# Gated cross-attention with a mixture of experts: seven half-size products for the experts' second layer, and two moves in the issue order

## The chip, the cores and the metric

The kernel runs on one core of a Trainium2 chip. The metric is device time in microseconds of one execution, given as the median of several runs. A core has five engines that each work through their own instructions in order and meet at semaphores: TensorE (PE in the profile, with its weight loads as PEld), VectorE (DVE), ScalarE (ACT), GpSimd (POOL) and SyncE (SP, which here only issues DMAs). All data is float32.

## The reference, cut to what matters

There are 4 x 1024 tokens of width 256, and a context of 64 rows for each of the 4 batches. The first half is a cross-attention with 16 heads of width 64, gated and added to x. The second half is a mixture of 8 experts with a hidden width of 1024: each token goes to its best two.

```python
# attention: per head, softmax(q k^T) v * q, then the projection
attn = softmax(einsum('hblk,hbmk->hblm', qh, kh))
out = einsum('hblm,hbmk->hblk', attn, vh) * qh
x = x + tanh(g_xattn) * (out.reshape(...) @ w_proj.T + b_proj)
# experts: top 2 of 8, weights from a softmax of the two logits
h = silu(einsum('td,edf->tef', xt, w1))      # 256 -> 1024
y = einsum('tef,efd->ted', h, w2)            # 1024 -> 256
x = x + tanh(g_ffn) * einsum('ted,te->td', y, combine)
```

The kernel computes only the two chosen experts of each token: tokens are sorted by expert into lists, and each run of list entries with one expert is a *slot*.

## The kernel before, in words

**Attention.** The tokens are cut into 8 groups (g = 0 to 7) of 512, a group into 4 tiles of 128. The main loop runs `for g in range(NG + 3): for t in range(T)`, and a pair (g, t) is called a step here. A step of the first eight groups issues the scores of its tile (`sc`, L385), the softmax (maximum L394, subtraction L396, exponential L399, sum L401, reciprocal L402, and the last multiplication `pr` on POOL, L404), and then the transposes of the *previous* step's probabilities (`pa`, L414). In step 1 of each group the attention product of the group before follows (`po`, L428, multiplied into `qT` on DVE at L437), in steps 2 and 3 its projection (`pp`, L445). Two groups later the second layer norm runs (`norm_again`), transposes `pt_b` (L281, copied by ACT at L286), the gate's logits `pl` (L467) and `pl_t` (L477).

**Routing.** After every second group, routing has found for each of 8 tiles of 128 tokens to which row of the lists its two entries go. `enter` writes them by indirect DMAs on POOL, two for a tile (L568). The function `entries(g, part)` issues 6 such writes at the last step of a group, 6 and 4 at the first two steps of the next. After the lists of groups 0 to 3 a table of *early* slots is made (slots 0 to 8), after those of groups 4 to 7 the table of *late* slots.

**Slots.** A generator, `run_slots`, issues the experts' work in small pieces; every `yield` ends one. For each slot s it gathers the tokens of slot s+3 (`gather_tokens`, POOL, L845), runs the hidden layer of slot s (`hidden`: `ph` on PE at L899, Silu on ACT at L907 into `hT`), transposes the tokens of slot s+1 (`transposed`: `pt` on PE, L867, copied by ACT to `xT`), and issues the second layer of slot s-1 (`combine`: products `py`, L978, with eviction and scaling on DVE, L966, an addition on POOL, L970, and a scatter to the output, L939; the output's old rows were gathered at L922). Loads of the next lists and weights are issued on SP between. Before the last slot's hidden layer, the second layer of the slot before it is issued. The table `pieces` says how many pieces go to which step of groups 6 to 10; what is left runs after the loop. `behind_softmax` puts a POOL instruction behind the newest multiplication `pr`.

Slots 0 to 8 hold 256 tokens. Of the late slots that run here, 9 to 15 hold 384 ("wide"), 16 to 20 hold 320 ("half": two tiles of 128 and one of 64) and 21 to 27 hold 256 ("plain"). A matmul call is for 128 columns of `hT` as weights and a row block of w2 (256 columns) as the moving operand; eight such calls, one for each 128 of the hidden width, make one tile of a slot's output. Each call leaves two records in the trace[...].

**Buffers.** PSUM has four single banks, handed out in turn by `bank(name)` (for `pt`, `pa`, `po`, `pp`, `pl`, `py` and others), and two double ones for scores and `ph`. The SBUF pool `soft`, tag "pr", has 2 buffers of 1024 float32 a partition; `npool`, tag "nT", has 4.

Of the kernel before, what the change touches and what calls it, by code (L numbers as in the profile page):

```python
# [8 lines left out]
F32 = mybir.dt.float32  # L9
I32 = mybir.dt.int32  # L10
AF = mybir.ActivationFunctionType
ALU = mybir.AluOpType
# [3 lines left out]
P = 128  # L16
# [5 lines left out]
def kernel(  # L22
# [13 lines left out]
    w2: bass.AP,  # L36
    out: bass.AP,
):

# [19 lines left out]
    nc = tc.nc  # L61
# [44 lines left out]
    def bank(name, spare=False):  # L106

        if spare:
            return ps2.tile([P, 2, 512], F32, tag="ps2", name=name)[:, 0]
        return ps1.tile([P, 512], F32, tag="ps1", name=name)  # L110
# [123 lines left out]
    def apart(tensor, dma, part=None, behind=()):  # L234

        writers = [writer for name in behind for writer in written[name]]
        tc.declare_no_dep(dma.ins, group=tensor, keep=writers, reason="different rows")
        tc.add_to_no_dep_group(tensor, dma.ins)
        for writer in writers:
            tc.add_manual_dep(  # L240
                dma.ins,
                writer.name,
                mybir.DependencyInfo(mybir.DependencyClass.Sync, mybir.DependencyReason.DATA),
                reason="rows of the part",
            )
        if part:
            written.setdefault(part, []).append(dma.ins)
# [589 lines left out]
    def behind_softmax():  # L837

        return tc.issue_after(newest[0]) if newest else nullcontext()
# [73 lines left out]
    def combine(s, ids, b, y, acc, hT):  # L913

        blocks = blocks_of(s)
        n = tokens_of(s)
        behind = [f"slot{s - 1}"] if s else ["out0"]
        if s == NA:
            behind.append("out1")
        for t, r in enumerate(blocks):  # L920
            with behind_softmax():
                gather = nc.gpsimd.indirect_dma_start(  # L922
                    out=acc[t][:r],
                    out_offset=None,
                    in_=outf[:n],
                    in_offset=bass.IndirectOffsetOnAxis(ap=ids[:r, t, 0:1], axis=0),
                    bounds_check=n - 1,
                    oob_is_err=False,
                )
            apart("out", gather, behind=behind)  # L930
        if attention_ends:
            py = [bank(f"py_{s}_{t}")[:, : D * r // P] for t, r in enumerate(blocks)]
        else:
            both = bank(f"py_{s}").rearrange("p (t d) -> p t d", d=D)
            py = [both[:, t, :] for t in range(blocks)]

        def scatter(t):
            r = blocks[t]
            put = nc.gpsimd.indirect_dma_start(  # L939
                out=outf[:n],  # L940
                out_offset=bass.IndirectOffsetOnAxis(ap=ids[:r, t, 0:1], axis=0),
                in_=acc[t][:r],
                in_offset=None,
                bounds_check=n - 1,
                oob_is_err=False,
            )
            apart("out", put, f"slot{s}")

        def parts_of(r):

            return [(slice(i * r, (i + 1) * r), slice(i * D * r // P, (i + 1) * D * r // P)) for i in range(P // r)]

        def add(t):
            r = blocks[t]
            last = s == NA + OFTEN - 1 and t == len(blocks) - 1
            if last:
                tc.keep_in_program_order(
                    nc.vector.scalar_tensor_tensor(
                        acc[t], py[t], ids.bitcast(F32)[:, t, 1:2], acc[t], ALU.mult, ALU.add
                    )  # L960
                )
                scatter(t)
                return

            for rows, columns in parts_of(r):
                evicted[s] = nc.vector.tensor_scalar(  # L966
                    y[t][:r, columns], py[t][rows], ids.bitcast(F32)[rows, t, 1:2], None, ALU.mult
                ).ins
            with behind_softmax():
                nc.gpsimd.tensor_tensor(acc[t][:r], acc[t][:r], y[t][:r], ALU.add)  # L970
                scatter(t)

        each = attention_ends
        per_tile = NF // len(hT)
        for t, r in enumerate(blocks):
            for f in range(NF):
                for rows, columns in parts_of(r):
                    nc.tensor.matmul(  # L978
                        py[t][rows],
                        hT[f // per_tile][:, f % per_tile, t * P : t * P + r],  # L980
                        b[:, f, columns],
                        start=(f == 0),
                        stop=(f == NF - 1),
                    )
            if each:
                add(t)
            yield
        if not each:
            for t in range(len(blocks)):
                add(t)  # L990
# [82 lines left out]
    def tabling(g):  # L1073

        nonlocal done, in_use
        if g == HG - 1:
            table, done = early_table()
            tables.append(table)
        elif g == NG - 1:
            table, in_use = late_table(done)  # L1080
            tables.append(table)

    def entries(g, part):
        nonlocal entered
        tiles = range(R)[3 * part : 3 * (part + 1)]
        with behind_softmax():
            enter(list(range(g - GB + 1, g + 1)), second["places"], tiles)
        entered += len(tiles)


    slots = run_slots(range(NA + OFTEN))
    pieces = {
        HG + 2: (0, 1, 1, 0), HG + 3: (3, 3, 2, 2), HG + 4: (3, 3, 3, 3), HG + 5: (1, 1, 2, 1), HG + 6: (1, 1),
    }
    last = None
    assert B * (H // 8) == 2 * T
# [12 lines left out]
    for g in range(NG + 3):  # L1109
        attention_ends = g >= NG  # L1110
        if g < NG:
            qT, aT = qTs[g], halves(f"aT_{g}", "hidden" if g % 2 and g + 1 < NG else "group")
            held[g] = (qT, aT)
        for h in parts[g]:
            if h == len(qTs):
                qTs.append(halves(f"qT_{h}"))
        before_last = g - 2
        ends = before_last % GB == GB - 1 and before_last >= 0
        for t in range(T):
            if g < NG:  # L1120
                pr = probabilities(g, t, qT)
            if last:
                transpose_probabilities(*last)
            if ends and t == 3:
                placing(before_last)
            products = [(h, p) for h, pairs in parts[g].items() for p in pairs[t]]
            if 0 < g <= NG and t == 1:
                for q in range(NP // 2):
                    attend(g - 1, q, *held[g - 1])
                    for h, p in products[q : q + 1]:  # L1130
                        queries(h, qTs[h], [p])
                products = products[NP // 2 :]
            for h, p in products:
                queries(h, qTs[h], [p])
            if 0 < g <= NG and t >= 2:
                project(g - 1, held[g - 1][0], (t - 2) * 2)
            last = (g, t, pr, aT) if g < NG else None
            if g == 0:
                for _ in range(value_parts[t]):
                    next(pending_values)  # L1140
            if 0 <= before_last < NG and t < 2:
                norm_again(before_last, t)
            if g + 2 < NG and t == 2:
                ln_norm(g + 2, stats, "a")
                add_bias(g + 2)
            if ends and t == 2:
                second["routing"] = route(second["logits"], f"{before_last}")
            if ends and t == 3:
                entries(before_last, 0)
            elif g >= GB + 2 and before_last % GB == 0 and t < 2:  # L1150
                entries(before_last - 1, t + 1)
                if t == 0:
                    tabling(before_last - 1)
            if g == 0 and t == 1:
                tc.keep_in_program_order(nc.scalar.activation(tg, tg, AF.Tanh))
                tc.keep_in_program_order(
                    nc.gpsimd.tensor_scalar(bias, bias, tg[:, 0:1], None, ALU.mult)
                )
                for h in range(2):
                    add_bias(h)  # L1160
            if g + 2 < NG and t == 0 and g % GB == 0:
                stats = ln_stats(list(range(g + 2, g + 2 + GB)), f"a{g + 2}")
            for _ in range(pieces[g][t] if g in pieces and t < len(pieces[g]) else 0):
                next(slots)
# [50 lines left out]
```

## Time and profile before

| what | value |
|---|---|
| time, median of 3 runs | 889.73 us (889.43 to 890.48) |
| the profiled execution's own time | 918.12 us |
| its span, from the first to the last instruction | 916.3 us |
| PE busy | 871.4 us (95%) |
| DVE, ACT, POOL busy | 327.8, 263.9, 403.0 us |
| second layer `py`, L978 | 1168 records, 238.3 us busy |
| hidden layer `ph`, L899 | 896 records, 233.8 us busy |
| list writes, L568 | 64, mean 971 ns |

The profiled execution took 28 us longer than the median of the timed runs, so a sum over its rows is a difference to itself, and how it carries over to the median has to be argued. PE is pipelined, so its busy time says that it had work, not that it ran at its peak. "Idle before" counts the time that an engine stood still just ahead of a group, with what released it. On the page, row 2 cuts the span into 40 slices of 22.9 us, and a digit is the busy share in tenths.

### The profile page before, as it was taken

How to read it: one execution, taken by the hardware profiler on the slowest of the kernel's cores; microseconds unless marked ns; L12 is line 12 of the kernel's file. 1: busy time of each engine (PE TensorE's matmuls, PEld its weight loads, DVE VectorE, ACT ScalarE, POOL GpSimd, SP SyncE). 2: the span in 40 equal slices, each digit the busy share in tenths (PEclk: the TensorE clock that was granted, in tenths of full speed). 3: DMA queues.
4: the chain of work that ended last, by engine and by line, in shares of the span. 5: the costliest groups of instructions: out<-in, count | busy, mean ns of one | idle time of the engine just before them, and what ended most of it. 6: DMA issues, size and time to landing. Idle time of an engine off the chain costs nothing.

```text
span 916.3 us, 11723 instructions
## 1 busy us (share of the span) xinstructions
PE 871.4 (95%) x4328; PEld 657.5 (72%) x4328; DVE 327.8 (36%) x729; ACT 263.9 (29%) x414; POOL 403.0 (44%) x392
## 2 busy tenths in 40 slices
PE   8999999999999998997997899999999999999995
PEld 5556858574857576865885787777777777888884
DVE  3467585777468748631155300000000001100010
ACT  4653353425242425432140121211211211121110
POOL 2051212146213553065447565555455555564443
PEclk9999999999999999998998899999999999999998
DMA  9600000001010225276372575744444564457111
GB/s 203 195 1 1 24 24 24 24 19 30 1 46 1 47 90 188 72 141 143 115 262 63 143 248 166 237 149 140 148 140 142 176 198 148 135 188 267 51 36 42
DMA packets 85279, 102.33 MB, mean 112 GB/s; under 512 B 29366, under 2 KB 71740, under 8 KB 85216
## 3 DMA queue, kind: packets, MB, share of 16 engines
q1 hardware_dynamic: 62656, 66.96, 24.4%
q0 software_dynamic: 11600, 25.25, 8.8%
q10 hardware_dynamic: 10960, 9.31, 3.7%
q8 instruction: 36, 0.59, 0.3%
q14 instruction: 27, 0.22, 0.1%
HBM read 84.75 MB, written 17.33 MB: 111 GB/s over the span
## 4 chain that ended last, share of the span: by engine, by line
PE 80%; DVE 10%; another core or an unknown queue 3%; issue 3%; DMA 1%; POOL 1%; ACT 1%; POOLq 0%; ACTq 0%; DVEq 0%
PE py L978 23%; PE ph L899 22%; PE pp L445 11%; PE pq L370 10%; PE sc L385 5%; PE pa L414 2%; PE pt L867 2%; PE po L428 2%; DVE qT L437 1%; PE pk L317 1%; DVE sm L401 1%; DVE pr L396 1%; DVE mx L394 1%; PE pt_b L281 1%
## 5 line engine op out<-in xcount | busy, mean ns | idle before, releaser
L978 PE MATMUL py<-w,hT 128*128 128x256 f32 (+1 forms) x1168 | 238.3, 369 | 9.2 <-issue 8.7
L899 PE MATMUL ph<-xT,w 128*128 128x256 f32 (+2 forms) x896 | 233.8, 418 | 2.1 <-ACT xT L872 1.2
L978 PEld LDWEIGHTS py<-w,hT 128*128 128x128 f32 (+1 forms) x1168 | 199.8, 184 | 40.2 <-issue 14.0
L899 PEld LDWEIGHTS ph<-xT,w 128*128 128x128 f32 x896 | 170.0, 191 | 57.5 <-issue 1.6
L907 ACT ACTIVATE hT<-ph 128x1024 f32<-128x1024 f32 (+3 forms) x84 | 69.9, 835 | 370.6 <-PE ph L899 319.5
L966 DVE TENSOR_SCALAR x<-py,ids 128x256 f32<-128x256 f32 (+1 forms) x72 | 33.5, 465 | 381.9 <-PE py L978 348.3
L404 POOL TENSOR_TENSOR pr<-pr,sm 128x1024 f32<-128x1024 f32 x32 | 60.9, 1902 | 218.1 <-DVE sm L402 202.1
L370 PE MATMUL pq<-nT_a,wq 128*128 128x512 f32 x256 | 117.0, 597 | 0.4 <-issue 0.2
L445 PE MATMUL pp<-wp,qT 128*128 128x256 f32 x512 | 113.2, 379 | 0.0
L445 PEld LDWEIGHTS pp<-wp,qT 128*128 128x128 f32 x512 | 97.0, 190 | 18.2 <-issue 5.3
L922 POOL DMA_INDIRECT x<-out_dram,ids x68 | 69.3, 1018 | 81.7 <-DMA out_dram<-x,ids 61.9
L845 POOL DMA_INDIRECT x<-normed,ids x68 | 67.9, 999 | 53.4 <-DMA ids<-lists 34.3
L970 POOL TENSOR_TENSOR x<-x,x 128x256 f32<-128x256 f32 (+1 forms) x67 | 48.3, 721 | 90.5 <-DVE x L966 77.8
L370 PEld LDWEIGHTS pq<-nT_a,wq 128*128 128x128 f32 x256 | 45.9, 190 | 53.5 <-issue 47.6
L939 POOL DMA_INDIRECT out_dram<-x,ids x68 | 69.0, 1015 | 23.2 <-POOL x L970 18.0
L568 POOL DMA_INDIRECT lists<-entry,to_row x64 | 62.1, 971 | 20.5 <-issue 17.9
L385 PEld LDWEIGHTS sc<-keys,qT 128*128 128x128 f32 x512 | 62.9, 192 | 7.9 <-issue 7.5
L385 PE MATMUL sc<-keys,qT 128*128 128x128 f32 x512 | 67.4, 278 | 0.0
L415 ACT COPY aT<-pa 128x512 f32<-128x512 f32 x64 | 34.6, 590 | 91.2 <-PE pa L414 71.1
L394 DVE TENSOR_REDUCE mx<-sc 128x16 f32<-128x1024 f32 x32 | 39.0, 1220 | 29.5 <-PE sc L385 28.3
L401 DVE TENSOR_REDUCE sm<-pr 128x16 f32<-128x1024 f32 x32 | 38.9, 1215 | 20.9 <-ACT pr L399 20.9
L377 ACT COPY qT<-pq 128x512 f32<-128x512 f32 x64 | 35.7, 582 | 28.4 <-PE pq L370 28.4
(209 smaller groups left out, 624.8 us busy)
## 6 DMA issues: line engine op xcount, KB each, us to landing
w<-in_L_ffn_w_dram SPq DMA_DIRECT2D x56, 1024.0 KB
out_dram<-x ACTq DMA_DIRECT2D x8, 512.0 KB
normed<-keep_b ACTq DMA_DIRECT2D x8, 512.0 KB
x<-in_x_dram SPq DMA_DIRECT2D x7, 512.0 KB
x<-normed,ids POOLq DMA_INDIRECT x68
x<-out_dram,ids POOLq DMA_INDIRECT x68
out_dram<-x,ids POOLq DMA_INDIRECT x68
wq<-in_L_xattn_w_qs_dram SPq DMA_DIRECT2D x4, 256.0 KB
```

The costliest lines, as they stand in the source:

```text
L370: nc.tensor.matmul(pq, wq[:, c, p * P : (p + 1) * P], nT[g][:, c, :], start=(c == 0), stop=(c == NC - 1),)
L385: nc.tensor.matmul(sc[:, p // 2, :, p % 2, :], of_pair(qT, p)[:, t * P : (t + 1) * P], kT[g // GB][:, p, :], start=True, stop=True,)
L404: nc.gpsimd.tensor_tensor(pr, pr, sm.unsqueeze(2).to_broadcast([P, H, M]), ALU.mult).ins
L445: nc.tensor.matmul(pp[:, i, :], of_pair(qT, p)[:, t * P : (t + 1) * P], wp[:, p, :], start=(p == 0), stop=(p == NP - 1),)
L568: nc.gpsimd.indirect_dma_start(out=lists, out_offset=bass.IndirectOffsetOnAxis(ap=to_row[:, k, i : i + 1], axis=0), in_=entry[:, k, i, :], ...
L845: gather = nc.gpsimd.indirect_dma_start(out=xin[t][:n], out_offset=None, in_=normed[: tokens_of(s)], in_offset=bass.IndirectOffsetOnAxis(a ...
L899: nc.tensor.matmul(ph[:, i, :], a[:, c, f * P : (f + 1) * P], xT[:, c, :], start=(c == 0), stop=(c == NC - 1),)
L907: nc.scalar.activation(hT[f0 // per_tile][:, f1 : f1 + step, :], ph, AF.Silu)
L922: gather = nc.gpsimd.indirect_dma_start(out=acc[t][:r], out_offset=None, in_=outf[:n], in_offset=bass.IndirectOffsetOnAxis(ap=ids[:r, t, 0 ...
L939: put = nc.gpsimd.indirect_dma_start(out=outf[:n], out_offset=bass.IndirectOffsetOnAxis(ap=ids[:r, t, 0:1], axis=0), in_=acc[t][:r], in_of ...
L970: nc.gpsimd.tensor_tensor(acc[t][:r], acc[t][:r], y[t][:r], ALU.add)
L978: nc.tensor.matmul(py[t][rows], hT[f // per_tile][:, f % per_tile, t * P : t * P + r], b[:, f, columns], start=(f == 0), stop=(f == NF - 1),)
```

## The change: what it does, and the diff

First, in slots 9 to 26 the two first tiles of the second layer (256 tokens x 1024 hidden by 1024 x 256) are cut into halves three ways: token tiles, the two halves of the hidden width, and the two halves of the output's columns. Eight products of quarter blocks become seven, by Winograd's form of Strassen's scheme: four sums of `hT` blocks (s1 to s4) and four of w2 blocks (t1 to t4) are made on DVE, seven products of four calls each at 128 columns go to one bank each, and the output's four blocks are put together from them on DVE by eight scaled additions, with two scaled copies on ACT. A third tile, where there is one, is done as before, and now ahead of the first two. Slot 27 is as before. The sums take buffers of the pools "pr" and "nT". The two POOL additions and scatters of the first two tiles come after product 3 and after product 4, the last.

Second, list writes: the tiles of a pair of groups go to a queue, `to_enter`, when their places are known, and each step takes one tile from it (two writes), or two tiles while the queue's first entry is of an odd-numbered pair of groups.

Third, `pieces`: the first pieces of the slots move one step on. In group 6 the generator's first two pieces go to steps 2 and 3 instead of 1 and 2; in group 7 the counts are (0, 4, 3, 3) instead of (3, 3, 2, 2). The totals are the same from the end of group 7 on.

```diff
+        whole = 2 if NA <= s < NA + OFTEN - 1 else 0
         if attention_ends:
-            py = [bank(f"py_{s}_{t}")[:, : D * r // P] for t, r in enumerate(blocks)]
+            py = [bank(f"py_{s}_{t}")[:, : D * r // P] if t >= whole else None for t, r in enumerate(blocks)]
...
+        def quarters():
+            half = NF // 2
+            if len(hT) == 2:
+                h = [[hT[k][:, :, i * P : (i + 1) * P] for k in range(2)] for i in range(2)]
...
+            w = [[b[:, k * half : (k + 1) * half, j * P : (j + 1) * P] for j in range(2)] for k in range(2)]
+            sums, more = (
+                soft.tile([P, 2, half, P], F32, tag="pr", name=f"{kind}_{s}") for kind in ("hsum", "wsum")
+            )
+            rest = npool.tile([P, 2, half, P], F32, tag="nT", name=f"rest_{s}")
+            s1, s2, s3, s4 = sums[:, 0], sums[:, 1], h[1][0], rest[:, 0]
+            t1, t2, t3, t4 = w[0][1], more[:, 0], rest[:, 1], more[:, 1]
+            for to, one, sign, other in (
+                (s1, h[1][0], ALU.add, h[1][1]),
+                (s3, h[0][0], ALU.subtract, h[1][0]),
+                (s2, s1, ALU.subtract, h[0][0]),
+                (s4, h[0][1], ALU.subtract, s2),
+                (t3, w[1][1], ALU.subtract, w[0][1]),
+                (t1, w[0][1], ALU.subtract, w[0][0]),
+                (t2, w[1][1], ALU.subtract, t1),
+                (t4, w[1][0], ALU.subtract, t2),
+            ):
+                nc.vector.tensor_tensor(to, one, other, sign)
...
+            def product(name, left, right):
+                to = bank(f"py_{s}_{name}")[:, :P]
+                n = NF // 2
+                for f in range(n):
+                    nc.tensor.matmul(to, left[:, f, :], right[:, f, :], start=(f == 0), stop=(f == n - 1))
+                return to
+
+            partial = work.tile([P, 2, P], F32, tag="xn", name=f"partial_{s}")
+            own = [y[i][:, j * P : (j + 1) * P] for i in range(2) for j in range(2)]
+
+            def plus(to, of, i, sofar):
+                evicted[s] = nc.vector.scalar_tensor_tensor(to, of, weight[i], sofar, ALU.mult, ALU.add).ins
+
+            p = product("1", h[0][0], w[0][0])
+            for i in range(2):
+                nc.scalar.activation(partial[:, i], p, AF.Copy, scale=weight[i])
+            p = product("2", h[0][1], w[1][0])
+            plus(own[0], p, 0, partial[:, 0])
+            fifth = product("5", s1, t1)
+            plus(own[1], fifth, 0, partial[:, 0])
+            p = product("7", s3, t3)
+            plus(own[2], p, 1, partial[:, 1])
+            p = product("6", s2, t2)
+            plus(own[1], p, 0, own[1])
+            plus(own[2], p, 1, own[2])
+            plus(own[3], fifth, 1, own[2])
+            p = product("3", s4, w[1][1])
+            plus(own[1], p, 0, own[1])
+            finish(0)
+            p = product("4", h[1][1], t4)
+            plus(own[2], p, 1, own[2])
+            finish(1)
+
+        def finish(i):
+            with behind_softmax():
+                nc.gpsimd.tensor_tensor(acc[i], acc[i], y[i], ALU.add)
+                scatter(i)
...
-    def entries(g, part):
+    to_enter = []
+
+    def entries():
         nonlocal entered
-        tiles = range(R)[3 * part : 3 * (part + 1)]
-        with behind_softmax():
-            enter(list(range(g - GB + 1, g + 1)), second["places"], tiles)
-        entered += len(tiles)
+        for _ in range(2 if to_enter and to_enter[0][0][0] // GB % 2 else 1):
+            if to_enter:
+                groups, places, tile = to_enter.pop(0)
+                with behind_softmax():
+                    enter(groups, places, [tile])
+                entered += 1
...
     pieces = {
-        HG + 2: (0, 1, 1, 0), HG + 3: (3, 3, 2, 2), HG + 4: (3, 3, 3, 3), HG + 5: (1, 1, 2, 1), HG + 6: (1, 1),
+        HG + 2: (0, 0, 1, 1), HG + 3: (0, 4, 3, 3), HG + 4: (3, 3, 3, 3), HG + 5: (1, 1, 2, 1), HG + 6: (1, 1, 0, 0),
     }
...
             if ends and t == 3:
-                entries(before_last, 0)
-            elif g >= GB + 2 and before_last % GB == 0 and t < 2:
-                entries(before_last - 1, t + 1)
-                if t == 0:
-                    tabling(before_last - 1)
+                groups = list(range(before_last - GB + 1, before_last + 1))
+                to_enter.extend((groups, second["places"], i) for i in range(R))
+            entries()
+            if g >= GB + 2 and before_last % GB == 0 and t == 0:
+                tabling(before_last - 1)
```

More of the change, by code (lines that the diff above doesn't have):

```diff
@@ L971, in add @@
                 scatter(t)
+        def quarters():
+            half = NF // 2
+            if len(hT) == 2:
+                h = [[hT[k][:, :, i * P : (i + 1) * P] for k in range(2)] for i in range(2)]
+            else:
+                h = [
+                    [hT[0][:, k * half : (k + 1) * half, i * P : (i + 1) * P] for k in range(2)]
+                    for i in range(2)
+                ]
+            w = [[b[:, k * half : (k + 1) * half, j * P : (j + 1) * P] for j in range(2)] for k in range(2)]
[16 more added lines that the diff above has]
+                nc.vector.tensor_tensor(to, one, other, sign)
+            return h, w, (s1, s2, s3, s4), (t1, t2, t3, t4)
@@ new lines, in seven_products @@
+        def seven_products(h, w, hsums, wsums):
+            s1, s2, s3, s4 = hsums
+            t1, t2, t3, t4 = wsums
+            weight = [ids.bitcast(F32)[:, i, 1:2] for i in range(2)]
+            def product(name, left, right):
[27 more added lines that the diff above has]
+            finish(1)
@@ L975, in combine @@
         for t, r in enumerate(blocks):
+            if t < whole:
+                continue
             for f in range(NF):
@@ L984, in combine @@
                     )
-            if each:
+            if each and not whole:
                 add(t)
+            yield
+        if whole:
+            operands = quarters()
+            for t in range(whole, len(blocks)):
+                add(t)
+            seven_products(*operands)
             yield
```

## The prediction

> **What bounds the kernel now.** I read the page first (parts 1 and 2), then the chain of waits, the groups by form, the waits of PE, and the timeline around the places that the change moves.
>
> ```profile
> span 916.3 us, 11723 instructions
> PE 871.4 (95%) x4328; PEld 657.5 (72%) x4328; DVE 327.8 (36%) x729; ACT 263.9 (29%) x414; POOL 403.0 (44%) x392
> PE   8999999999999998997997899999999999999995
> DVE  3467585777468748631155300000000001100010
> ```
>
> TensorE is busy for 95% of the span, in nearly every slice; VectorE is close to idle from the middle on (digits 0 and 1). So a change is worth what it takes from PE's stream or adds to its idle time. The page's PEclk row is 9 almost throughout.
>
> The chain of waits shows the late stage as nothing but PE. Its columns are start, length, what:
>
> ```profile
> 336.82 1.78 PE sc L385 x16
> ...
> 836.08 6.91 PE py L978 x32
> 842.98 6.91 PE ph L899 x32
> 849.89 0.44 PE pt L867 x4
> 850.33 6.91 PE py L978 x32
> ```
>
> A plain slot (256 tokens) costs 6.91 (first layer, ph), 0.44 (transposes, pt) and 6.91 (second layer, py): 14.26 us without a gap. Every matmul call leaves two records, so py's 32 records are 16 calls, 216 ns a record at 256 columns. The scores sc are the same instruction at 128 columns: 1.78/16 = 111 ns.
>
> PE's waits, with engine and releaser, total, times, longest:
>
> ```profile
> PE pl L467 <- ACT nT_b L286: 6.5, 1, 6.5
> ...
> PE ph L899 <- ACT xT L872: 1.2, 1, 1.2
> PE pa L414 <- POOL pr L404: 1.1, 2, 0.7
> ```
>
> All PE gaps over 0.1 us sum to some 31 us. The 6.5 us wait and about 10 us of gaps at 491-508 us, together with a PE clock of half rate after each (0.76 on average from 415 to 429 us), make about 22-24 us. I take them as most of what lies between this execution (918.12 us: span 916.3 and 1.8 around it) and the timed median of 889.73. My sum is a difference against the profiled execution's rows; I carry it to the median unchanged, since none of its terms sits in those two stretches.
>
> **Part 1, seven products.** For 18 late slots (9 to 26; `whole`) the first two 128-token tiles lose 2 x 8 calls at 256 columns and get 7 products x 4 calls at 128. Removed: 32 records, 6.91 us. Added: 56 records x 111 ns = 6.22 us. Gain 0.69 us a slot, x18 = **-12.5 us**. Third tiles of wide and half slots and slot 27 stay.
>
> A rule of the Trainium skill speaks against this. "TensorE: Matmul & The Clock Gate", section "Back-to-back issue gap", gives a sustained stream of load-and-multiply pairs 81 ns at 128 columns and 131 at 512: a quarter of the columns for 0.62 of the time, because the weight load sets a floor. Between those, 256 columns come to about 98 (my estimate on that page's line), so 56 x 81 = 4.54 against 32 x 98 = 3.13: 1.4 us *more* a slot, +25 us in all. Here the ratio is 111 to 216, almost one half; sc's x16 and, in the timeline below, its x32 hold it. I take the trace, as it has the very shape and type.
>
> The extra vector work: eight sums of 128x512 a slot and eight scaled adds of 128x128, in place of two scalings of 128x256. Nearest rows:
>
> ```profile
> L966 DVE TENSOR_SCALAR x<-py,ids 128x256 f32<-128x256 f32 x62 | 30.0, 484 | 374.2 <-PE py L978 342.3 <-DMA x<-out_dram,ids 13.9 <-issue 5.9
> ...
> L329 ACT COPY keys<-pk 64x128 f32<-64x128 f32 x32 | 6.0, 264 | 1.7 <-PE pk L317 1.6
> ...
> L490 DVE TENSOR_TENSOR cmp<-lg 128x512 f32<-128x512 f32 x4 | 2.7, 687 | 4.4 <-PE pa L414 4.4
> ```
>
> 8 x 0.69 = 5.5 us, and 8 x 0.35 = 2.8 (the 64x128 scaling off PSUM, also L966, takes 349 ns), less 2 x 0.48: +7.3 us of DVE a slot, 132 in all, and two ACT copies of 0.27-0.3. Cover: L966 alone stood idle 374 us, and the sums need only hT and the weights, which are ready before the next slot's hidden phase of 6.91 us ends. Following the semaphores through a wide, a half, a plain and the last pair of slots, I find no product that waits: product 7 needs s3, the second sum made; product 4 needs product 7's bank, emptied two products (1.8 us) before. Cost taken: 0. If the cover fails (DVE late by one sum at each slot) it is 0.69 x 18 = 12.5, which just eats the gain; below nothing it cannot go.
>
> **Part 2, the tail.** Both POOL adds and scatters of a slot now follow products 3 and 4, at the end, where before tile 0's ran half a slot early. At slots 25 and 26 this delays the chain scatter, gather (2.4-2.9 us each in the chain after 885 us), add, scatter that ends at slot 27's last row. Of the 1.4 us that the last two slots gain, about 0.9 comes back: **+0.9** (0 to +1.4).
>
> **Part 3, the first pieces a step later.** Here is what group 7's first steps lose:
>
> ```profile
> 351.03 3.74 PE L385 MATMUL sc<-keys,qT 128*128 128x128 f32 x32
> ...
> 355.94 3.72 PE L899 MATMUL ph<-xT,w 128*128 128x256 f32 x16 [1.17 <-ACT xT L872]
> ...
> 357.35 1.16 DVE L401 TENSOR_REDUCE sm<-pr 128x16 f32<-128x1024 f32 x1
> 357.60 1.90 POOL L404 TENSOR_TENSOR pr<-pr,sm 128x1024 f32<-128x1024 f32 x1 [9.97 <-DVE sm L402]
> ...
> 359.55 1.09 PE L414 MATMUL pa<-ident,pr 128*128 128x128 f32 x8
> ...
> 374.88 3.40 PE L445 MATMUL pp<-wp,qT 128*128 128x256 f32 x15
> ```
>
> PE fills the wait for the first softmax of group 7 (steps 0 and 1) with slot 0's transposes and half its hidden phase: pt and two ph pieces, 0.6 + 3.72 us. In the changed order sc of both steps stands back to back and pa follows with nothing between. The softmax is DVE's chain (max 1.2, subtract 1.2, sum 1.2 twice over), so pa can't come earlier: by the order on DVE the reciprocal that POOL waits for falls behind the second step's sum, pa at 360.7 instead of 359.55, and PE stands idle from about 357 to 360.7. The work taken out is done later, in steps where PE was full. Stepping on with before's durations: po, then pl and pl_t with their copies, then ph_0 after its xT copy (0.5-0.9 us of wait each, as no other work lies between), pp of step 2 starts near 378.8 instead of 374.88, with 1.73 of ph and 0.55 of pt still owed and 0.67 of sc done early: 3.9 + 2.3 - 0.7 = 5.5; and slot 1's xT copy now stands right before its ph: 0.8. Sum **+6.3** (from +3, if the waits overlap better than in my hand order, to +9).
>
> Does the gap bring the half clock? The trace has one clear case: idle 415.35 to 421.83, and a mean clock of 0.76 for 415-429. The same page, section "What's actually happening", says that one idle window of about 3.4 us is enough and that one busy window restores it. By the rule 3.7 us idle costs 2-4 us; by the trace only 6.5 us is shown to. I weight it by about a third: **+0.7**.
>
> **Part 4, list writes.** Sixty-four writes, 971 ns each on POOL, go from 6+6+4 tiles to one or two a step. What could wait is the softmax multiply on POOL queued behind them, and PE for it: L414's 1.1 us in all, so at most -1. In turn the second batch ends about 13 us later (near 340); the id loads and first token gathers then fall at 345-356, just ahead of the multiply at 358.7. Cost **0** (to +3 if a gather slips behind that multiply's slot and slot 0's transposes wait). The later batches come out as one run of sixteen as now, so they are not relieved.
>
> **Sum.** -12.5 + 0.9 + 6.3 + 0.7 + 0 = -4.6; 889.73 - 4.6 = **885.1 us**.
>
> **Rivals.**
> A. *Forecast*: PE saves by columns, group 7's gap gives half back. 882-888.
> B. *The gap is cheap* (other work slides in, later idle absorbs it): -12.5 + 0.9 + 0 to 3: about 879. For it: PE had 10 us of scattered idle already. Against: the order on PE is fixed, and nothing lies between sc and pa.
> C. *Slower: the half clock settles in behind group 7's gap.* The idle stretch throttles PE and each short wait after it (xT, qT, nT copies) keeps it throttled. In 355-375 us PE does 17.75 us of work now; less the 4.3 that moves away, 13 us at half rate cost 13, of which some 4 lie inside waits for DVE: +9, and 6.3 + 9 + 0.9 - 12.5 = +3.7: 893.4. It decides from 5.3 us of half-clock loss, two windows' worth. For it: PE's other long gap has the half clock behind it. Against: that gap was nearly twice as long.
> D. *Slower: weight loads or the seven groups' boundaries set the products' pace.* It decides at 6.91 - 7.9/18 = 6.47 us a slot, 116 ns a record. At 130 ns it is 7.28, +0.37 x 18 + 7.9 = +14.6: 904; at the page's ratio 923. For it: seven chains of eight records in place of two of sixteen. Against: sc runs at 111 in chains of two.
> E. *The products do nothing they promise*, since DVE is late by one sum a slot: -12.5 + 12.5 + 7.9 = +7.9: 897.6. Against: VectorE's idle digits.
>
> **How the numbers follow.** A 0.5, B 0.15, C 0.18, D 0.07, E 0.1. What can be told from no change is about 0.2% here, 1.8 us. Faster: B and most of A, 0.6; same: A's upper edge and the mildest C, 0.13; slower: 0.27. The range 878 to 897 takes in A, B, C and the most of E; D lies outside. A's own range is 882-888.
>
> **What would show it.** In the chain after, x56 of the products in 6.2 us between ph x32; no idle before them; DVE's late digits at 2-5, near +130 us busy. PE idle at the first softmax of group 7 (about 3-4 us, waiting for POOL pr) and several short waits for ACT and DVE behind it. The clock there tells the half-rate term. Wrong if products take over 6.47 us, if PE waits for DVE in each slot (E), or if group 7 shows no gap (B).

## The result and the profile after

The changed kernel takes 885.99 us (median of six runs, 885.46 to 886.76) against 889.71 for the kernel before (six runs). The ratio is 0.9958, with a 95% interval of 0.9945 to 0.997: faster by 3.7 us, some 0.4%. The forecast was 885.1. The first four kernels below ran on another chip, where every execution, the kernel before's too (918.1 us), lay some 28 us higher and scattered by 2 to 3%; all later ones ran where the kernel before takes 889 to 892.

From the page of the changed kernel:

```profile
span 884.1 us, 12970 instructions
PE 852.7 (96%) x4760; PEld 659.2 (75%) x4760; DVE 459.6 (52%) x981; ACT 269.4 (30%) x446; POOL 416.1 (47%) x392
PE   7999999999999999799999999999999999999995
DVE  3466484787558675654128400544344455646460
```

VectorE has 131.8 us more to do than before, and its late digits are now 3 to 6 (the last slice, behind the products, apart). Between its first and last slice PE is at 9 in all but one, the 17th (354-376 us), which holds group 7.

A plain slot in the timeline (start, length, engine, line, what):

```profile
832.38 0.60 PE L870 MATMUL pt<-ident,x 128*128 128x128 f32 x4
...
832.82 1.95 PE L1021 MATMUL py<-w,hT 128*128 128x128 f32 x16
834.60 1.06 PE L1021 MATMUL py<-w,hsum 128*128 128x128 f32 x8
835.50 1.06 PE L1021 MATMUL py<-rest,hT 128*128 128x128 f32 x8
836.39 1.06 PE L1021 MATMUL py<-wsum,hsum 128*128 128x128 f32 x8
837.28 1.06 PE L1021 MATMUL py<-w,rest 128*128 128x128 f32 x8
838.18 1.06 PE L1021 MATMUL py<-wsum,hT 128*128 128x128 f32 x8
839.07 7.07 PE L902 MATMUL ph<-xT,w 128*128 128x256 f32 x32
```

The products follow one another without a gap: from 832.82 to 839.07 it is 6.25 us for 56 records, 111.6 ns each, and the next slot's transposes start 13.60 us after this one's (14.26 before).

PE's waits (total, times, longest), and the same stretch of group 7 that was shown of before:

```profile
PE pa L417 <- POOL pr L407: 4.2, 3, 3.1
...
PE ph L902 <- ACT xT L875: 2.5, 2, 1.8
...
PE py L1021 <- DVE x L1029: 0.2, 1, 0.2
```

```profile
348.41 4.05 PE L388 MATMUL sc<-keys,qT 128*128 128x128 f32 x32
353.10 2.02 PE L388 MATMUL sc<-keys,qT 128*128 128x128 f32 x16 [0.64 <-DVE pr L399]
...
356.19 3.85 POOL L407 TENSOR_TENSOR pr<-pr,sm 128x1024 f32<-128x1024 f32 x2 [3.71 <-DVE sm L405]
358.19 1.97 PE L417 MATMUL pa<-ident,pr 128*128 128x128 f32 x8 [3.07 <-POOL pr L407]
```

Three steps' scores stand nearly back to back, then PE is idle for 3.07 us until POOL's multiplication is done. In all 18 slots only one wait of the products for a vector result is long enough to be listed, 0.2 us. The granted clock, the third number from the end of a row in a view by windows, fell at 357.26 us, inside that idle stretch:

```profile
357.00:364.00 7.00, 5.81 (x28) 2.89 (x32) 6.13 (x7) 2.23 (x3) 5.09 (x4) 0.52 1.07 382
```

It was half until 364.09 us, for almost the whole window.

### The profile page after: what moved, and what is told of

Same layout as the page of the kernel before. It is cut to its first block, busy times and chain, and to the rows that moved or that the text cites. A ratio compares the mean times of both kernels' runs of the same rounds, so it can differ in the third digit from the quotient of the medians.

```text
span 884.1 us, 12970 instructions
## 1 busy us (share of the span) xinstructions
PE 852.7 (96%) x4760; PEld 659.2 (75%) x4760; DVE 459.6 (52%) x981; ACT 269.4 (30%) x446; POOL 416.1 (47%) x392
## 5 line engine op out<-in xcount | busy, mean ns | idle before, releaser
L902 PEld LDWEIGHTS ph<-xT,w 128*128 128x128 f32 x896 | 168.2, 190 | 56.0 <-ACT xT L875 2.9
L925 POOL DMA_INDIRECT x<-out_dram,ids x68 | 72.9, 1071 | 91.6 <-DMA out_dram<-x,ids 72.8
L1063 PE MATMUL py<-w,hT 128*128 128x256 f32 (+1 forms) x592 | 106.6, 352 | 0.0
L1063 PEld LDWEIGHTS py<-w,hT 128*128 128x128 f32 (+1 forms) x592 | 89.5, 176 | 11.3 <-issue 0.3
L848 POOL DMA_INDIRECT x<-normed,ids x68 | 70.5, 1036 | 31.9 <-issue 19.8
L943 POOL DMA_INDIRECT out_dram<-x,ids x68 | 73.3, 1077 | 22.8 <-POOL x L1053 9.8
L1004 DVE TENSOR_TENSOR w<-w 128x512 f32<-128x512 f32 x18 | 12.9, 718 | 90.8 <-PE py L1063 90.6
L970 DVE TENSOR_SCALAR x<-py,ids 128x256 f32<-128x256 f32 (+1 forms) x36 | 16.0, 443 | 84.5 <-PE py L1063 84.3
L455 DVE SCALAR_TENSOR_TENSOR x<-pp,tg,x 128x512 f32<-128x512 f32 x16 | 12.0, 749 | 70.3 <-PE pp L448 70.3
```

Of the source, the lines that this page charges most:

```text
L848: gather = nc.gpsimd.indirect_dma_start(out=xin[t][:n], out_offset=None, in_=normed[: tokens_of(s)], in_offset=bass.IndirectOffsetOnAxis(a ...
L902: nc.tensor.matmul(ph[:, i, :], a[:, c, f * P : (f + 1) * P], xT[:, c, :], start=(c == 0), stop=(c == NC - 1),)
L925: gather = nc.gpsimd.indirect_dma_start(out=acc[t][:r], out_offset=None, in_=outf[:n], in_offset=bass.IndirectOffsetOnAxis(ap=ids[:r, t, 0 ...
L943: put = nc.gpsimd.indirect_dma_start(out=outf[:n], out_offset=bass.IndirectOffsetOnAxis(ap=ids[:r, t, 0:1], axis=0), in_=acc[t][:r], in_of ...
L1063: nc.tensor.matmul(py[t][rows], hT[f // per_tile][:, f % per_tile, t * P : t * P + r], b[:, f, columns], start=(f == 0), stop=(f == NF - 1),)
```

## The experiments

**The parts, one by one, on the disturbed chip.** Four kernels: the products alone; the later pieces alone; the spread writes alone with the loads that they force a step later; and the changed kernel with group 7's counts of before.

```diff
# writes_spread (without the products) and seven_writes, against the changed kernel
-        HG + 2: (0, 0, 1, 1), HG + 3: (0, 4, 3, 3), ...
+        HG + 2: (0, 0, 1, 1), HG + 3: (3, 3, 2, 2), ...
# seven_only: entries(g, part) and pieces as before
# pieces_later: the kernel before with the changed kernel's pieces
```

> The kernel before with the seven products alone: list writes and pieces as before. If the products save by columns (56 records at 111 ns in place of 32 at 216) and the end loses little: -12.5 + 0.3, about 877.5 us, with no PE gap between group 7's scores and its transposes beyond the 1.2 us of before. If products pay at their boundaries or for late sums, it stays above 880.

Measured: 910.7 us, ratio 0.9933 (0.9907 to 0.996).

> The kernel before with the later pieces alone. If group 7's gap, with its half clock, is what gives the gain back: +8.2 us as read off the two traces from group 7's first scores to slot 2's transposes, about 898 us. If the gap is absorbed later or the half clock is an accident of the profile, +3 to +6: 893 to 896.

Measured: 934.6 us, ratio 1.0217 (1.0148 to 1.0286).

> The kernel before with the spread list writes alone. Since the lists are complete a step later, the first two pieces (loads, first gathers) stay at steps 2 and 3 of group 6; group 7 has the counts of before (3, 3, 2, 2). If the two microseconds by which the changed kernel's trace is ahead at group 6 come from the writes: about 887.6 us. If they are an accident of the profiled execution: 889.7 (no change).

Measured: 922.0 us, ratio 1.007 (1.0038 to 1.0102).

> The changed kernel with group 7's piece counts of before (3, 3, 2, 2) and the rest of the change kept. If the three parts add up: -12.5 - 2.1 + 0.3, about 875.4 us. If the end of the kernel is now bound by the chain of scatters and gathers and not by PE, part of the 2 us is lost: 876 to 878.

Measured: 916.6 us, ratio 1.000 (0.9971 to 1.0029).

The signs fit (products gain, later pieces lose, spread writes gain nothing), the sizes don't. PE's gaps in these traces sum to some 25 to 34 us from 190 us on (14 in the changed kernel's first trace), 10 to 16 us of it at 410-430 and 495-515 us, and the clock is half for 24 to 38 us before the tail (6.83 in that trace). So each size is mixed with stalls that no part of the change explains, and what follows from them is no more than the signs.

**The parts on an undisturbed chip**, with the changed kernel beside them.

> The changed kernel itself, beside its parts on one chip. If the undisturbed timing of the two kernels is what counts: ratio 0.996 to before. If this chip shows the same long stalls behind group 7 as the one where the parts ran (all times there lie some 28 us higher): the ratio is smeared by some tenths of a per cent.

Measured: 886.57 us, ratio 0.9959 (0.9945 to 0.9973).

> Seven products alone, once more, for the sum of parts on the chip of the changed kernel. If products save by columns: 12 us under before, 0.9865. If half of that is lost to something that the product's own stage doesn't show: 0.993, as measured among the disturbed runs.

Measured: 879.92 us, ratio 0.9877 (0.9862 to 0.9892), between the two expectations but with the first inside its interval. This is the best version measured: it beats the changed kernel by 6.7 us.

> The changed kernel with group 7's counts of before (3, 3, 2, 2). Against the changed kernel it gives the price of the later pieces (8 us by the traces, so 878 or 0.987 of before); against seven products alone the price of the spread writes with the first loads and gathers a step later. If the first gathers now come too late for slot 0's transposes (a wait of 3.9 us for them stood in its trace), it is 2 to 4 us slower than seven products alone; if the writes' 2 us and this cancel, equal.

Measured: 884.09 us, ratio 0.9928 (0.9915 to 0.9942): 4.2 us slower than the products alone, and 2.5 faster than the changed kernel. In its timeline the first gathers of tokens come late:

```profile
343.68 1.90 POOL L407 TENSOR_TENSOR pr<-pr,sm 128x1024 f32<-128x1024 f32 x1 [4.53 <-DVE sm L405]
...
347.30 1.07 POOL L848 DMA_INDIRECT x<-normed,ids  x1 [1.72 <-DMA ids<-lists]
...
355.09 0.90 PE L870 MATMUL pt<-ident,x 128*128 128x128 f32 x3 [4.52 <-DMA x<-normed,ids]
```

With the products alone the same first gather starts at 336.07, a multiplication earlier, and nothing waits:

```profile
336.07 1.07 POOL L848 DMA_INDIRECT x<-normed,ids  x1 [1.82 <-DMA ids<-lists]
...
350.33 0.60 PE L870 MATMUL pt<-ident,x 128*128 128x128 f32 x4
```

The profiled execution of this kernel was the slowest of its five (886.8), so 4.5 us is likely the upper end of that wait. The wait has a second price. The clock fell to half at 353.53 us, during it, and stayed there for 6.83 us; the scores behind the transposes, here and then with the products alone, are the same 32 records:

```profile
355.79 5.92 PE L388 MATMUL sc<-keys,qT 128*128 128x128 f32 x32
...
350.77 3.74 PE L388 MATMUL sc<-keys,qT 128*128 128x128 f32 x32
```

So 2.2 us of the loss in this trace are the half clock's, beside the 4.5 of the wait.

**Is it the spread, or the step's delay of the loads?** The products alone, with nothing but the first two pieces a step later:

```diff
-        HG + 2: (0, 1, 1, 0), HG + 3: (3, 3, 2, 2), ...
+        HG + 2: (0, 0, 1, 1), HG + 3: (3, 3, 2, 2), ...
```

> Seven products alone, with the first two pieces (loads of ids and weights, first gathers) a step later in group 6, list writes as before. If it is the step's delay that makes slot 0's transposes wait for their gathered tokens: pt waits 4 to 5 us and the time is 4 us over seven products alone, 0.9925 of before. If it is the spread writes that hold the loads up on POOL's queue: as seven products alone, 0.988.

Measured: 882.9 us, ratio 0.9912 (0.9899 to 0.9926), 0.35% over the products alone. Its first gather starts at 345.32, since `behind_softmax` now holds it behind the multiplication that ends at 345.2; slot 0's transposes wait 2.1 us for tokens (4 to 5 were expected), and behind that the 32 score records take 5.36 us in place of 3.74, the clock being half for 3.41 us from 352.85 on (this profiled execution, too, was the slowest of its kernel, 886.9). So most of the loss comes from the step. Spreading may add about 1 us (884.09 against 882.9), but these are two chips and the intervals overlap, so that is not shown. The traces fit it: there the gather starts at 347.30, waiting for `ids`, whose load follows the last list write by 5.5 to 6.2 us in all three kernels, and with spread writes the last one ends later.

**Does the half clock cost anything of its own?** The changed kernel, with work that nothing reads put into the gap:

```diff
 def transpose_probabilities(g, t, pr, aT):
+        if (g, t) == (HG + 3, 0):
+            spare = bank("spare")
+            for _ in range(16):          # 34 in the second kernel
+                nc.tensor.transpose(spare[:, :P], ident, ident)
```

> The changed kernel with 16 needless transposes of the identity (3.6 us of PE work, nothing reads them) set between group 7's second and third scores, where PE else stands idle before the first softmax is done. The wait for the softmax stays. If the half clock behind the idle stretch costs something of its own: the clock stays at 1.0 from 357 to 364 us and the time falls by 1 to 2.3 us. If only the waits count (DVE's evictions pace that stretch anyway): no change, within 0.5.

Measured: 886.27 us, ratio 0.9961 (0.9946 to 0.9975). The 16 transposes took only 1.91 us: a transpose leaves one record, not two as a product does. 2.6 us of the gap were left and the clock fell as before, so this told nothing.

> The changed kernel with 34 needless transposes in group 7's gap (16 left 2.6 us of it, and the clock still fell). Now about 0.7 us of idle time is left. If the half clock has its own price: the clock stays at 1.0, the first attention products take 4.8 us in place of 5.5, and slot 2's transposes come 1 to 2 us sooner after the first scores of group 7 than in the changed kernel (58.0 us). If not: 58 us within 0.3.

Measured: 887.83 us, ratio 0.9969 (0.9956 to 0.9981). Windows of it (PE, PE loads, DVE, ACT, POOL busy, then clock, DMA share, GB/s):

```profile
357.00:368.00 11.00, 8.63 (x66) 4.18 (x64) 10.30 (x14) 3.04 (x5) 7.24 (x5) 1.00 0.90 320
368.00:372.00 4.00, 2.17 (x25) 1.39 (x18) 1.83 (x4) 0.76 (x2) 0.36 (x1) 0.99 0.54 143
372.00:376.00 4.00, 4.00 (x13) 3.18 (x12) 0.00 (x0) 0.91 (x1) 0.00 (x0) 0.58 0.29 119
```

The clock stayed whole behind the gap, and the attention products still waited for VectorE, which is busy for 10.30 of 11 us there. Slot 0's transposes came 23.9 us after group 7's first scores. In the changed kernel it is 23.4 in the trace of `changed_again`, where the clock was half for 3.41 us, and 24.1 in its first trace, where it was half for 6.83. But this kernel differs from the changed one in more than its clock: eight of the score records that lay ahead of the gap run here behind the transposes `pt_b` (from 367.01 us on), so it doesn't isolate the clock. The two traces of the changed kernel do, being of one program. There VectorE works from the softmax's sums on (353.5 us in the first trace) until the last product is multiplied, and in between it stood idle for an attention product three times, twice in the first trace and once, the last line, in `changed_again`:

```profile
362.12 1.29 DVE L440 TENSOR_TENSOR qT<-po,qT 128x512 f32<-128x512 f32 x2 [0.45 <-PE po L431]
363.83 1.29 DVE L440 TENSOR_TENSOR qT<-po,qT 128x512 f32<-128x512 f32 x2 [0.42 <-PE po L431]
...
363.66 2.48 DVE L440 TENSOR_TENSOR qT<-po,qT 128x512 f32<-128x512 f32 x4 [0.30 <-PE po L431]
```

So behind this gap the half clock costs at most 0.9 us where it lasts 6.83 us and 0.3 where it lasts 3.41: VectorE sets the pace. In `gap_filled_2` the clock fell later instead, at 371.95, where PE is full: the next 24 records of `ph` took 7.13 us in place of 5.45, and slot 2's transposes came after 60.2 us in place of 58.0.

**Are the sums under cover?** The products alone with four of the eight sums made twice.

```diff
-                nc.vector.tensor_tensor(to, one, other, sign)
+                for _ in range(2 if any(to is x for x in (s2, s4, t2, t4)) else 1):
+                    nc.vector.tensor_tensor(to, one, other, sign)
```

> Seven products alone with four of the eight sums (s2, s4, t2, t4) made twice: 2.4 us more of VectorE's time a slot, the same numbers. If the sums lie under cover: in plain slots, where VectorE stands idle for 4.5 us ahead of the first product's eviction, no change (13.60 us a slot); in wide and half slots, where the sums of the weights come only after the third tile's products, 0 to 0.5 us a slot for the 1.2 us added there: 880 to 886 in all. If VectorE sets the pace of the products (the rival by which sums are late at each slot): 2.4 us on each of 18 slots, over 920.

Measured: 878.65 us, ratio 0.989 (0.9864 to 0.9915), as the products alone. Its page and its largest wait of a product:

```profile
PE 849.5 (97%) x4760; PEld 658.2 (75%) x4760; DVE 508.1 (58%) x1053; ACT 274.5 (31%) x450; POOL 425.8 (49%) x392
...
PE py L1022 <- DVE wsum L1005: 1.3, 1, 1.3
```

47 us more of VectorE's work (508.1 against 460.7) cost one wait of 1.3 us; the plain slots still take 13.60.

**The kernel before, for a second trace.**

> The kernel before once more, for a trace without the long stalls at 415-421 and 491-508 us of its first one. If those stalls are what the first profiled execution had over the median: a span near 888 us, PE's gaps from 190 us on down to some 9 us. If it always shows them under the profiler: again near 916.

Measured: one execution, 891.03 us, whose trace is free of the long stalls.

```profile
span 889.3 us, 11723 instructions
PE 861.4 (97%) x4328; PEld 654.4 (74%) x4328; DVE 327.3 (37%) x729; ACT 263.6 (30%) x414; POOL 405.0 (46%) x392
```

Its PE gaps from 190 us on sum to 9.6 us, against 27.5 in the first trace, whose clock was also half for 6.83 us from 419.17 and for 13.65 us from 497.68 on, which costs up to 10.2. Together that is the 28 us, so they were stalls of that execution, and differences are better read off this one. The first profiled execution took what the kernel before takes on the disturbed chip (918.12 against a median of 918.08 us) and stalls in the same two stretches; whether it ran there is not on record.

## Why the prediction was right, point by point

With four undisturbed traces PE's time can be cut at marks that all share: the first scores of group 7, slot 2's transposes, slot 9's transposes (the last before the first slot with products is combined), and PE's end. In us:

| stretch | `before_clean` | `seven_only_b` | `seven_writes_b` | `changed_again` |
|---|---|---|---|---|
| group 7 to slot 2 | 50.54 | 50.54 | 57.16 | 58.03 |
| slot 2 to slot 9 | 124.67 | 124.74 | 123.95 | 123.55 |
| slot 9 to PE's end | 357.27 | 345.79 | 345.80 | 345.81 |

Changed less before: +7.5, -1.1, -11.5, in all -5.1 from group 7's first scores on. The two executions also differ by +1.1 us ahead of group 7 and by -0.2 in the tail, which makes the -4.2 between their spans; the timed medians say -3.7.

- *Products, -12.5 forecast.* Measured -11.5 on PE. The mechanism was right; a slot takes 6.25 us and not 6.22, so 0.66 x 18 = 11.9, and 0.4 us of waits stand in the last pair of slots, where no hidden phase lies between. The trace's row decided rightly against the 81 and 131 ns that the Trainium skill, "TensorE: Matmul & The Clock Gate", section "Back-to-back issue gap", gives for 128 and 512 columns: 128 columns take 111.6 ns a record here, 256 take 216.
- *Cover for VectorE, 0 forecast.* Shown: added sums of 47 us changed nothing (rival E falls). The 132 us of added work were forecast, and 131.8 came, in part by luck: the sums took 0.79 us each on average and not 0.69, and VectorE's instructions overlap a little.
- *Tail, +0.9 forecast.* Not found. From PE's end to the span's end it was 10.5 us in the undisturbed trace of before and is 10.3 now. The chain did slip against PE, but by 0.5 us: the last gather starts 4.2 us ahead of PE's end before and 3.7 now. The gather then took less time, here before and then in the changed kernel's first trace, with PE's end at 878.82 and 873.80:

```profile
879.21 0.48 DVE L958 SCALAR_TENSOR_TENSOR x<-py,ids,x 128x256 f32<-128x256 f32 x1 [3.32 <-DMA x<-out_dram,ids]
...
874.03 0.48 DVE L962 SCALAR_TENSOR_TENSOR x<-py,ids,x 128x256 f32<-128x256 f32 x1 [3.17 <-DMA x<-out_dram,ids]
```

VectorE's last addition follows the gather's start by 4.6 us before and by 3.9 now, so it comes just behind PE's end in both. Why this gather is quicker is not shown.

- *Group 7, +6.3, and the half clock, +0.7.* The gap came where it was forecast (3.7 us idle forecast, 3.07 + 0.64 measured), with the short waits for xT behind it (0.68 and 1.78). The stretch cost 7.5, of which 1.1 came back by slot 9. The half clock came too, in every trace of the changed kernel, against my weight of a third. That weight passed over a second case in the trace of before: the clock had fallen at 497.68 us behind two gaps of 1.5 us each and shorter ones. Nor is it a matter of one whole idle window of about 3.4 us, as the Trainium skill has it (same page, section "What's actually happening"): the gap here is 3.07 us long, and in `gap_filled` 2.60 were enough. The 2 to 4 us that I gave a half clock where it happens are what failed: in this stretch it cost at most 0.3 to 0.9 us, since VectorE sets its pace. That the term came out near its 0.7 is luck, a cost put too high times a chance put too low.
- *List writes, 0 forecast, to +3 if a gather slips.* In the changed kernel the gathers do lie just ahead of the multiplication (344.9 to 352.5, then 356.2), so nothing waits for them. But I had put the price of the step's delay on group 7's order alone. `seven_writes_b` shows that with group 7's old counts the late loads cost 4.2 us by themselves, in a wait for tokens and a half clock behind it, and the counts of the changed kernel add 2.5. The two are one cost, 6.7 us, not two: in the orders measured, who delays the loads by a step pays either a wait for tokens at `pt` or a gap with nothing in it. The 2 us by which the changed kernel's first trace seemed to gain before group 7 are not there between `changed_again` and `before_clean`.

Of the rivals, B (a cheap gap) and D (the products' pace) are refuted by the trace rows above, and C's mechanism came without C's price. The total came out within 1 us partly because the errors cancel: the products were forecast 1.0 too high, the tail 1.1 too costly, group 7 with its clock 0.5 too cheap, and 1.1 us won back before slot 9 was not seen at all. Two of the prediction's readings of the trace of before were short as well, without weight in the sum: PE's gaps there come to 34.4 us and not 31, and what lies between that execution and the median is the whole 28 us of stalls and half clock, not 22 to 24.

What stays open is what the long stalls on the one chip, and in the first trace of before, come from: in the first trace of before PE, VectorE and ScalarE all stand idle from 416 to 420 us while GpSimd is busy for 3.09 of these 4 us, and the chain of waits names "another core or an unknown queue".

## What to carry to other kernels

A matmul scheme with fewer multiplications pays on a kernel bound by PE as soon as the narrow products run at the rate by columns and the additions fit beside other PE work: read both off rows of the same shape before writing it. A change in the order of a small producer (here list writes, worth nothing) can force its consumers a step later, and that step was worth more than half of the gain: price the delay at the consumer, in every order that the consumer can take. A half clock on PE costs where PE sets the pace (2.2 us on 32 score records behind the wait for tokens) and little where another engine does (at most 0.3 to 0.9 us behind group 7's gap).

## What the runs showed of the hardware that had not been expected

The clock also fell without one long idle stretch: in `gap_filled_2` at 371.95 us, behind four microseconds in which PE was busy for 2.17 and its longest gap was 1.16. It stayed low for 3.41 us there. In `loads_later` it fell at 352.85 behind two waits of 1.29 and 0.84 us. In all traces the lengths are multiples of 3.41 us, but for the last one of each, in the tail: 3.41 in `changed_again`, 6.83 in the first trace of the changed kernel, 6.83 and 13.65 in the first trace of before. A transpose leaves one record of 109 ns and a product of the same size two, so filler work sized in calls came out at half of what was meant.
